# Two scrap tiles, transfers in halves and refitted costs in the planner of a four-layer graph network

## The chip, the cores and the metric

One Trainium2 chip, one core. The time is device microseconds for one execution of the whole program: 2293.68 us before, the median of 3 runs (2291.74 to 2293.85).

## The reference

Thirty-two graphs of 512 nodes with 256 features each (`x`), and a dense 512 x 512 adjacency matrix for each (`adj`), all float32. Four layers run one after the other on each graph; each ends in a residual and a LayerNorm over the features:

```
x = LN(x + gin(x, adj))       # (1+eps) x + adj x, @W1 (256->512), relu, @W2 (512->256)
x = LN(x + gcn(x, adj))       # adj (x W^T + b), leaky with alpha
x = LN(x + graphconv(x, adj)) # h = LN(x); x + relu((adj h) W_rel + b_rel + h W_root)
x = LN(x + gin3(x, adj))      # eps x + adj x, @W1 (256->1024), RMSNorm, silu, @W2 (1024->256)
```

The graphs do not depend on each other. Within a graph nearly everything is one long chain: aggregate, multiply, normalise, and again.

## The kernel before

**Recorded operations.** The kernel does not issue instructions as it walks through the layers. Each helper (`mm`, `act`, `total`, `add`, `copy`, `move` and so on) records an operation in a `Plan` (class at L281), with the tiles that it reads and writes. Because every operation is issued by one closure, all compute instructions carry L366 in the profile and all DMAs L413; tiles tell them apart, not lines.

**The products.** Aggregation (four per graph), both wide layers and most of the narrowing layers are done by a seven-product scheme (`seven`, L846): seven block products into PSUM banks instead of eight, with sums of blocks made on VectorE before, and results added from PSUM to SBUF by VectorE or copied by ScalarE. So VectorE has nearly as much to do as TensorE. A float32 matmul shows as two records.

**The tiles.** SBUF holds 37 `room` tiles of 128 x 1024 (L679), which the planner hands out and takes back; PSUM is eight banks named `ps`; `few` tiles hold the norms' columns. A norm takes, for each of the four chunks of 256 columns of a matrix, a sum (Identity) and a sum of squares (Square) on ScalarE: `Norm.half` (L1177) calls `total` (L735) for them. Only the accumulated column is wanted; the 128 x 256 elementwise output goes to one constant tile `scrap` (L836), which every such operation writes.

**The second layer's bias.** ScalarE writes the bias times the row sum straight into a PSUM bank ahead of the matmuls that accumulate on it (L1421, "seed" in what follows): four 128 x 256 operations per graph.

**The turns.** Where a layer's output comes out transposed (layer 0 in graphs 3 to 28, layer 3 in graphs 1 to 28), VectorE transposes 32 x 32 blocks ("squares") and `spread_squares` (L1272) moves them through DRAM: four writes of 128 KB into a `corner` buffer, then one read of 512 KB back into a room, which VectorE adds to the residual (`add_turned`, L1131). `gather_squares` (L1285) does the like for layer 2, with four writes and four reads of 128 KB. Results leave in one transfer of 512 KB for all but the last two graphs (L1503), which leave in two of 256 KB.

**The order.** `Plan.order` (L479) is a list scheduler that runs when the kernel is built. Up to five graphs are in flight. It gives each operation a rank, which is the graph's number times a period (37) with a shift of its own for some graphs (`SHIFT`), plus when TensorE will need the operation (scaled by a pace, 1.8); the last three graphs follow at 19 instead of 37. Then, step by step, it takes the engine that can start something first, and of what can start there the operation of the lowest rank. When something "can start" comes from a table of assumed costs in us, fitted by hand: busy time and tail of each kind of instruction (L33 to L64), of each kind of DMA (L83 to L87: wire time, and time until landed), a margin `SPARE` after a landing, and a hand-over `HAND` per engine (L93), the time between an instruction's end on one engine and the start of one that waits for it on another. Copies and the scaling at a norm's end may go to VectorE or ScalarE: the planner takes the one that ends first, with `YIELD` (L113) added to VectorE's end. All DMAs go through SyncE's queue in the planner's order; an issue waits until the one eight before has landed (`LANES`). The order within each engine is then fixed, and semaphores do the rest: an instruction that is not ready holds up all that stand behind it on its engine.

Of the kernel before, what the change touches and what calls it, by code (L numbers as in the profile page):

```python
# [12 lines left out]
AF = mybir.ActivationFunctionType  # L13
ALU = mybir.AluOpType

P = 128
# [5 lines left out]
def span(ap):  # L22

    n = 1
    for d in ap.shape[1:]:
        n *= d
    return n
# [28 lines left out]
    return 0.035 + n * 0.00089 + columns * 0.113, 0.105  # L56


def total_time(n, columns):
    return 0.187 + n * 0.00089 + columns * 0.1, 0.1  # L60

# [8 lines left out]

SPARE = 0.8


KEEP = 0.4
# [3 lines left out]
    return 0.1 + kbytes / 450, 1.0  # L80


LOAD, BLOCK = (0.9, 1.7), (0.3, 0.67)  # L83
KEPT, BACK = (0.2, 0.6), (0.35, 0.93)
CORNER, PIECES = (0.46, 0.8), (0.65, 1.05)
TURNED, QUARTER = (2.1, 0.63), (0.58, 0.98)
LINE, SPREAD, RESULT = (0.22, 0.1), (1.47, 0.81), (1.36, 0.8)  # L87

GENTLE = 2.7

HAND = dict(tensor=0.12, vector=0.09, scalar=0.09, gpsimd=0.14, sync=0.1)  # L93
WEIGHTS, AGAIN = 0.09, 0.09


# [13 lines left out]
SOON = 0.03  # L110


YIELD = 0.6  # L113

# [2 lines left out]

RULES = [(37, 1.8, 19, 0.7)]

SHIFT = {-1: -19, 0: 12, 1: 3, 2: 2, 3: -1, 5: 1, 30: -8, 31: -18}
HALVES = 2
AHEAD, LAST = 86.0, 500.0
TURN = {0:(2,3),2:(99,0),3:(0,3)}
ROWS = 1  # L130
ONE = 0
# [149 lines left out]
class Plan:  # L281
# [60 lines left out]
    def do(self, out, *ways, ordered=None, scrap=None, behind=()):  # L342


        ins = list(behind)
        port = False
        def first(x):
            ap = x.model if isinstance(x, Part) else x
            return ap.offset // ap.ap[0][0] if ap.ap[0][0] else 0
        crosses = False  # L350
        for e, method, _, args, kw in ways:
            tiles = [x for x in (*args, *kw.values()) if isinstance(x, (bass.AP, Part))]
            ins += tiles
            in_psum = any(isinstance(x, Part) and x.room.pool.psum for x in tiles)
            crosses |= e == "vector" and any(first(x) != first(out) for x in tiles)
            port |= e == "gpsimd" or method in TWO_OPERANDS and not in_psum

        def issue(engine, method, args, kw):
            def put(x):
                return x.place() if isinstance(x, Part) else x  # L360

            kw = {k: put(x) for k, x in kw.items()}
            if scrap is not None:
                kw["accum_out"] = put(out)
            to = put(out) if scrap is None else scrap
            getattr(getattr(self.nc, engine), method)(to, *(put(x) for x in args), **kw)  # L366

        self.add(
            {
                e: (times, lambda e=e, m=method, args=args, kw=kw: issue(e, m, args, kw))  # L370
                for e, method, times, args, kw in ways
            },
            out, ins, ordered, port, crosses=crosses,
        )
# [267 lines left out]
def tile_gnn_stack(ctx: ExitStack, tc: tile.TileContext, a: dict, out: bass.AP):  # L642
# [33 lines left out]
    HC = NC // 2  # L676
    TH = N // 2
    FH = FC3 // 2
    FLIGHT, ROOMS, SMALL = 5, 37 - ONE, 10  # L679

    const = ctx.enter_context(tc.tile_pool(name="const", bufs=1))
    work = ctx.enter_context(tc.tile_pool(name="work", bufs=1))
# [37 lines left out]
    def scalar(func, n, x, times=scalar_time, **kw):  # L720
        columns = sum(k in ("scale", "bias") and not isinstance(v, float) for k, v in kw.items())
        return "scalar", "activation", times(n, columns), (x,), dict(func=func, **kw)
# [10 lines left out]
        plan.do(o, scalar(func, span(o), x, **kw))  # L733

    def total(o, x, func, **kw):  # L735
        plan.do(o, scalar(func, span(x), x, times=total_time, **kw), scrap=scrap)

    def copy(o, x):
        plan.do(o, scalar(AF.Copy, span(o), x), vector("tensor_copy", span(o), x))
# [38 lines left out]
    def bank(*shape, onto=False, sums=True):  # L778

        n = 1
        for d in shape:
            n *= d
        return Part(Room(banks, sums=n * sums, onto=n * onto)).shaped(*shape)
# [4 lines left out]
    def half(t, h):  # L790
        return t[:, h * HC : (h + 1) * HC]
# [16 lines left out]
    def constant(name, shape):  # L808
        return const.tile(shape, F32, tag=name, name=name)
# [23 lines left out]
    ident = constant("ident", [P, P])  # L833
    make_identity(nc, ident)
    mhalf = constant("mhalf", [P, N // Q])
    scrap = constant("scrap", [P, D])  # L836
    nc.vector.memset(scrap, 0.0)
    nc.vector.memset(mhalf, -0.5)
    pause = constant("pause", [P, 48])
    nc.vector.memset(pause, 0.0)  # L840
# [324 lines left out]
    class Norm:  # L1165
# [33 lines left out]
        def finish(self, h, m, plus, place):  # L1199

            mine = slice(h * HC, (h + 1) * HC)
            ve, rstd, shift = self.ve[:, mine], self.rstd[:, mine], self.shift[:, mine]
            ts(ve, self.squares[:, mine], m / self.n, plus, ALU.mult, ALU.add)
            inv_sqrt(rstd, ve)
            mul(shift, self.less[:, mine], rstd)
            for c in range(h * HC, (h + 1) * HC):
                self.put(c, self.r, rstd[:, c % HC : c % HC + 1], shift[:, c % HC : c % HC + 1])
            plan.move(place, half(self.r, h), (RESULT[0] / 2, RESULT[1]), into=f"out{plan.graph}{h}")

        def put(self, c, y, scale, shift):  # L1210
            r = self.r[:, c, :]
# [60 lines left out]
    def spread_squares(of):  # L1272

        to = room(P // Q, NC * DC * Q)
        of, via = of.whole(P // Q, NC * DC * Q), next(corners)
        names = [f"{via.tensor.name}{a}" for a in range(P // Q)]
        places = via.rearrange("(b i) (a x) -> a i b x", i=Q, a=P // Q)
        for a, name in enumerate(names):  # L1280
            plan.move(places[a], of[a * Q : (a + 1) * Q], CORNER, into=name)
        plan.move(to.whole(N * DC), via, TURNED, outof=names)
        return to

    def gather_squares(to, of):  # L1285
# [64 lines left out]
    def load_x(b):  # L1350
        x = tok()
        src = a["x"][b].rearrange("(p c) d -> p c d", c=NC)
        for h in range(2):
            plan.move(half(x, h), half(src, h), LOAD, gentle=b > 0)
        return x

    def aggregate_first(x, adjacency):
# [40 lines left out]
    def layer1(x, adjacency):  # L1398

        rows = adjacency.row_sums()  # L1400
        aT = aggregate(x, adjacency)
        rs = small(NC)
        by_token(rs, column_sums(rows), 1.0, None, ALU.mult)
        v, neg = tok(), tok()
        norm = Norm(v)

        def done(h):
            act(half(neg, h), half(v, h), AF.Relu, scale=-1.0)
            stt(half(x, h), half(neg, h), nalpha, half(x, h), ALU.mult, ALU.add)
            stt(half(v, h), half(v, h), 0.0, half(x, h), ALU.max, ALU.add)  # L1410
            norm.half(h)

        if ONE:
            for c in range(NC):
                act(v[:, c, :], b_1, AF.Copy, scale=rs[:, c : c + 1])
            dense_add(v, dense_sums(*([halves(aT[:, k : k + 1])] for k in range(DC))), A_1, done, "one")
        for h in range(0 if ONE else 2):
            if SEED:
                ps = dense_tok(
                    [(aT[:, k, :], W_1[:, k, :]) for k in range(DC)], h,  # L1420
                    lambda o, c: plan.do(o, scalar(AF.Copy, D, b_1, scale=rs[:, c : c + 1]), behind=[aT] if BEHINDS else []),  # L1421
                )
                got = ps
            else:
                ps = dense_tok([(aT[:, k, :], W_1[:, k, :]) for k in range(DC)], h)
                for i in range(HC):
                    c = h * HC + i
                    stt(v[:, c, :], b_1, rs[:, c : c + 1], ps[:, i, :], ALU.mult, ALU.add)
                got = half(v, h)
            act(half(neg, h), got, AF.Relu, scale=-1.0)  # L1430
            stt(half(x, h), half(neg, h), nalpha, half(x, h), ALU.mult, ALU.add)
            stt(half(v, h), got, 0.0, half(x, h), ALU.max, ALU.add)
            norm.half(h)

        norm.scales((1.0 + LN_EPS, LN_EPS * LN_EPS), (0.25, 0.25 * LN_EPS))
        h = norm.scaled(0)
        xx = norm.scaled(1)
        u = tok()
        for c in range(NC):
            if ROWS:  # L1440
                act(u[:, c, :], shift_rel, AF.Copy, scale=rs[:, c : c + 1])
            else:
                stt(u[:, c, :], shift_rel, rs[:, c : c + 1], shift_2, ALU.mult, ALU.add)
        if ROWS:
            plus_row(u, shift_2)
        return h, xx, u
# [21 lines left out]
    def layer3(x, adjacency, b):  # L1468
# [27 lines left out]
        if b < B - HALVES:  # L1496
            if turn:
                add_turned(x, dense_turned(right, A2_3, b2c_3), norm.half)
            else:
                dense_add(x, right, A2_3, norm.half)  # L1500
            norm.scales((1.0, LN_EPS))
            y = norm.scaled()
            plan.move(place, y, RESULT, into=f"out{b}", gentle=b < B - 4)  # L1503
        else:

            def done(h):
                norm.half(h)
                norm.finish(h, 1.0, LN_EPS, half(place, h))

            dense_add(x, right, A2_3, done)  # L1510
# [1 line left out]


    plan.graph = -1
    idle, zeros = bank(D), scrap
    for _ in range(9):
        mm(idle, zeros[:, 0:P], zeros, True, True)
    eps0 = row("L0_gnn_eps")
# [2 lines left out]
    loop0 = constant("loop0", [P, P])  # L1521
    ts(loop0, ident, one_eps0, None, ALU.mult)
    plan.graph = 0
    x = load_x(0)
    adjacency = Adjacency(0)
    W1_0 = weight("L0_gnn_W1")
# [83 lines left out]
```

## Time and profile before

| what | value |
|---|---|
| median of 3 runs | 2293.68 us |
| the profiled execution, its own time | 2292.24 us |
| its span, first to last instruction | 2290.4 us |
| granted TensorE clock, mean | 0.999 |
| busy TensorE / VectorE / ScalarE / GpSimd | 2275.2 / 2121.8 / 1762.2 / 240.5 us |
| HBM traffic | 84 GB/s over the span |

A row of a group of instructions reads: line, engine, operation, tile written <- tiles read, shape, count, then busy time, mean duration in ns, and idle time of the engine just before with what ended it. PE is TensorE's matmul, PEld its weight load, DVE VectorE, ACT ScalarE, SPq SyncE's DMA queue. A norm's accumulating operation appears as two records, an ACTIVATE and an ACTIVATION_READ_ACCUMULATOR. Matmuls overlap, so durations add up to more than the time; what counts is the distance from one start to the next.

### The profile page before, as it was taken

The page shows a single profiled execution, that of the slowest core. Times are in us where ns is not written, and L with a number is a line of the kernel's source. Part 1 is how long each engine was busy: PE and PEld are TensorE (multiplying, and loading weights), DVE is VectorE, ACT ScalarE, POOL GpSimd, SP SyncE. Part 2 cuts the span into 40 slices and gives each one's busy share as a digit, 9 for nine tenths or more (in the row PEclk, how much of TensorE's full clock was granted, in tenths as well). Part 3 has the DMA queues.
Part 4 walks back from the last instruction along what each step waited for, and adds up shares of the span by engine and source line. Part 5 has one row for each costly group of instructions (what it writes and reads, how often), then busy time and mean ns, then how long its engine had stood idle before and what let it go on. Part 6 is the DMA issues. An engine that isn't in the chain of part 4 may idle for free.

```text
span 2290.4 us, 37068 instructions
## 1 busy us (share of the span) xinstructions
PE 2275.2 (99%) x11694; PEld 2012.6 (88%) x11694; DVE 2121.8 (93%) x5404; ACT 1762.2 (77%) x4733; POOL 240.5 (11%) x168
## 2 busy tenths in 40 slices
PE   9999999999999999999999999999999999999998
PEld 8889888888888888888888888888888888888888
DVE  8989998999999999999999999999999999998988
ACT  4777778777787777877778877778777887768785
POOL 0000101111011110111100111101111011101111
PEclk9999999999999999999999999999999999999999
DMA  8011322243321333323333223332133331333101
GB/s 246 26 31 40 106 83 75 69 111 106 105 71 54 109 107 106 85 52 94 111 96 112 46 80 111 106 104 77 49 109 109 86 106 51 95 90 84 42 15 61
DMA packets 268404, 195.71 MB, mean 85 GB/s; under 512 B 144560, under 2 KB 224176, under 8 KB 268208
## 3 DMA queue, kind: packets, MB, share of 16 engines
q1 hardware_dynamic: 268208, 193.35, 29.6%
q8 instruction: 93, 1.52, 0.3%
q14 instruction: 103, 0.84, 0.1%
HBM read 124.27 MB, written 69.01 MB: 84 GB/s over the span
## 4 chain that ended last, share of the span: by engine, by line
PE 82%; DVE 8%; ACT 5%; DMA 2%; issue 1%; SPq 1%; POOLq 0%; POOL 0%; DVEq 0%; ACTq 0%
PE ps L366 82%; DVE room L366 7%; ACT room L366 3%; ACT scrap L366 2%; DMA room<-corner 1%; SPq L413 1%; DMA corner<-room 1%; DVE few L366 0%; ACT ps L366 0%; DMA room<-in_x_dram 0%; DVE few L391 0%; DVE A L366 0%; DMA line<-few 0%; POOLq L1606 0%; DVE pause L1571 0%
## 5 line engine op out<-in xcount | busy, mean ns | idle before, releaser
L366 PE MATMUL ps<-room,room 128*128 128x256 f32 (+1 forms) x3572 | 925.9, 381 | 3.5 <-DVE room L366 1.9
L366 DVE TENSOR_TENSOR room<-room,room 128x512 f32<-128x512 f32 (+1 forms) x1486 | 852.1, 601 | 14.7 <-ACT room L366 7.0
L366 PE MATMUL ps<-room,L_gnn_W 128*128 128x256 f32 x2848 | 751.7, 380 | 1.9 <-DVE room L366 1.7
L366 PEld LDWEIGHTS ps<-room,room 128*128 128x128 f32 x3572 | 654.0, 190 | 94.7 <-ACT room L366 8.0
L366 PEld LDWEIGHTS ps<-room,L_gnn_W 128*128 128x128 f32 x2848 | 535.6, 190 | 81.5 <-DVE room L366 5.7
L366 DVE TENSOR_TENSOR room<-ps,room 128x256 f32<-128x256 f32 (+1 forms) x1125 | 528.2, 485 | 70.3 <-PE ps L366 64.6
L366 PE MATMUL ps<-room,A 128*128 128x256 f32 x2136 | 563.6, 379 | 0.3 <-ACT room L366 0.2
L366 ACT ACTIVATE room<-ps,L_gnn_b_c 128x256 f32<-128x256 f32 x984 | 409.8, 469 | 73.6 <-PE ps L366 71.4
L366 POOL TENSOR_TENSOR few<-few,mhalf 128x4 f32<-128x4 f32 (+2 forms) x162 | 239.8, 1481 | 2045.4 <-DVE few L366 1680.8
L366 PEld LDWEIGHTS ps<-room,A 128*128 128x128 f32 x2136 | 403.5, 190 | 56.4 <-ACT room L366 1.9
L366 ACT ACTIVATE room<-ps 128x256 f32<-128x256 f32 (+1 forms) x577 | 227.6, 400 | 244.2 <-PE ps L366 239.2
L366 DVE TENSOR_TENSOR room<-room 128x256 f32<-128x256 f32 (+1 forms) x638 | 311.3, 494 | 16.6 <-ACT room L366 7.3
L366 ACT ACTIVATE scrap<-room,few 128x256 f32<-128x256 f32 x500 | 253.3, 507 | 67.5 <-DVE few L366 61.7
L366 ACT ACTIVATE room<-room,few 128x256 f32<-128x256 f32 x464 | 252.2, 595 | 29.1 <-DVE few L366 28.8
L366 ACT ACTIVATE scrap<-room 128x256 f32<-128x256 f32 x500 | 207.4, 415 | 52.7 <-DVE room L366 43.3
L366 ACT ACTIVATE room<-room 128x1024 f32<-128x1024 f32 x192 | 202.3, 1057 | 48.6 <-DVE room L366 47.6
L366 PE MATMUL ps<-L_gnn_W,room 128*128 128x256 f32 (+1 forms) x960 | 207.6, 331 | 0.7 <-DVE room L366 0.6
L366 ACT ACTIVATE room<-room,L_gnn_rms_weight_c 128x512 f32<-128x512 f32 x256 | 171.7, 722 | 4.2 <-DVE room L366 4.1
L366 PEld LDWEIGHTS ps<-L_gnn_W,room 128*128 128x128 f32 x960 | 156.4, 191 | 17.3 <-ACT ps L366 1.3
L366 PE MATMUL ps<-A,room 128*128 128x128 f32 x1104 | 155.4, 276 | 0.5 <-DVE room L366 0.4
L366 PEld LDWEIGHTS ps<-A,room 128*128 128x128 f32 x1104 | 147.5, 191 | 8.9 <-DVE room L366 2.4
L366 DVE STREAM_TRANSPOSE room<-room 128x512 f32<-128x512 f32 x168 | 113.8, 696 | 1.6 <-ACT room L366 0.5
(62 smaller groups left out, 1221.2 us busy)
## 6 DMA issues: line engine op xcount, KB each, us to landing
corner<-room SPq DMA_DIRECT2D x336, 128.0 KB, 2.5
room<-in_adj_dram SPq DMA_DIRECT2D x128, 256.0 KB, 5.6
room<-corner SPq DMA_DIRECT2D x54, 512.0 KB, 3.8
room<-in_x_dram SPq DMA_DIRECT2D x64, 256.0 KB, 5.8
room<-corner SPq DMA_DIRECT2D x120, 128.0 KB, 3.0
out_dram<-room SPq DMA_DIRECT2D x30, 512.0 KB, 4.7
room<-in_adj_dram SPq DMA_DIRECT2D x128, 64.0 KB, 2.0
diagonal<-room SPq DMA_DIRECT2D x62, 128.0 KB, 2.1
```

The lines of the kernel that those rows point to most:

```text
L366: getattr(getattr(self.nc, engine), method)(to, *(put(x) for x in args), **kw)
L413: getattr(self.nc, engine).dma_start(to, of, **kw)
```

## The change

- `scrap` becomes two tiles, and each accumulating operation takes the next one at the moment at which it is issued, so they alternate in the order in which ScalarE runs them.
- The 512 KB read of a turn becomes two of 256 KB, one for each half of the columns; the first needs only the first two of the four writes. The 512 KB results become two of 256 KB.
- A new cost `seed_time` for the seeds: 0.115 us more than other ScalarE operations.
- 36 rooms instead of 37.
- The assumed costs and the scheduler's constants change: DMA figures, x loads with a figure of their own, 0.05 more in every entry of `HAND`, `SPARE` 1 for 0.8, `YIELD` 0.3 for 0.6, the spacing of the last graphs, `SHIFT`, `AHEAD`.

No operation of the computation is added or dropped. Since the scheduler runs on the new figures, the order changes on every engine.

```diff
+def seed_time(n, columns):
+    return 0.15 + n * 0.00089 + columns * 0.113, 0.105
...
-SPARE = 0.8
+SPARE = 1
...
-LOAD, BLOCK = (0.9, 1.7), (0.3, 0.67)
-KEPT, BACK = (0.2, 0.6), (0.35, 0.93)
-CORNER, PIECES = (0.46, 0.8), (0.65, 1.05)
-TURNED, QUARTER = (2.1, 0.63), (0.58, 0.98)
-LINE, SPREAD, RESULT = (0.22, 0.1), (1.47, 0.81), (1.36, 0.8)
+LOAD, LOAD_X, BLOCK = (0.86, 1.8), (0.67, 1.4), (0.3, 0.66)
+KEPT, BACK = (0.31, 0.5), (0.33, 0.94)
+CORNER, PIECES = (0.43, 0.84), (0.61, 1.09)
+TURNED, QUARTER = (0.75, 1.05), (0.59, 1.05)
+LINE, SPREAD, RESULT = (0.22, 0.1), (1.45, 0.83), (0.66, 1.1)
...
-HAND = dict(tensor=0.12, vector=0.09, scalar=0.09, gpsimd=0.14, sync=0.1)
+HAND = dict(tensor=0.17, vector=0.14, scalar=0.14, gpsimd=0.19, sync=0.15)
...
-YIELD = 0.6
+YIELD = 0.3
...
-RULES = [(37, 1.8, 19, 0.7)]
+RULES = [(37, 1.8, 15, 0.3)]
...
-SHIFT = {-1: -19, 0: 12, 1: 3, 2: 2, 3: -1, 5: 1, 30: -8, 31: -18}
+SHIFT = {-1: -22, 0: 12, 1: 3, 2: 2, 4: -1, 5: -3, 30: -4, 31: -5}
 HALVES = 2
-AHEAD, LAST = 86.0, 500.0
+AHEAD, LAST = 72.0, 500.0
...
-            to = put(out) if scrap is None else scrap
+            to = put(out) if scrap is None else next(scrap)
...
-    FLIGHT, ROOMS, SMALL = 5, 37 - ONE, 10
+    FLIGHT, ROOMS, SMALL = 5, 36, 10
...
-    scrap = constant("scrap", [P, D])
-    nc.vector.memset(scrap, 0.0)
+    scraps = [constant(f"scrap{i}", [P, D]) for i in range(2)]
+    nc.vector.memset(scraps[0], 0.0)
...
-        plan.move(to.whole(N * DC), via, TURNED, outof=names)
+        for h in range(2):
+            mine = slice(h * N * DC // 2, (h + 1) * N * DC // 2)
+            plan.move(to.whole(N * DC)[:, mine], via[:, mine], TURNED, outof=names[2 * h : 2 * h + 2])
...
-            plan.move(half(x, h), half(src, h), LOAD, gentle=b > 0)
+            plan.move(half(x, h), half(src, h), LOAD_X, gentle=b > 0)
...
-            plan.move(place, y, RESULT, into=f"out{b}", gentle=b < B - 4)
+            for h in range(2):
+                plan.move(half(place, h), half(y, h), RESULT, into=f"out{b}{h}", gentle=b < B - 4)
...
+    scraps = cycle(scraps)
```

More of the change, by code (lines that the diff above doesn't have):

```diff
@@ L735, in total @@
     def total(o, x, func, **kw):
-        plan.do(o, scalar(func, span(x), x, times=total_time, **kw), scrap=scrap)
+        plan.do(o, scalar(func, span(x), x, times=total_time, **kw), scrap=scraps)
     def copy(o, x):
@@ L1207, in finish @@
                 self.put(c, self.r, rstd[:, c % HC : c % HC + 1], shift[:, c % HC : c % HC + 1])
-            plan.move(place, half(self.r, h), (RESULT[0] / 2, RESULT[1]), into=f"out{plan.graph}{h}")
+            plan.move(place, half(self.r, h), RESULT, into=f"out{plan.graph}{h}")
         def put(self, c, y, scale, shift):
@@ L1420, in layer1 @@
                     [(aT[:, k, :], W_1[:, k, :]) for k in range(DC)], h,
-                    lambda o, c: plan.do(o, scalar(AF.Copy, D, b_1, scale=rs[:, c : c + 1]), behind=[aT] if BEHINDS else []),
+                    lambda o, c: plan.do(o, scalar(AF.Copy, D, b_1, times=seed_time, scale=rs[:, c : c + 1]), behind=[aT] if BEHINDS else []),
                 )
@@ L1514, in tile_gnn_stack @@
     plan.graph = -1
-    idle, zeros = bank(D), scrap
+    idle, zeros = bank(D), scraps[0]
     for _ in range(9):
```

## The prediction

> **What bounds the kernel now.** I read the page's shares first, then the table of stretches, then TensorE's timeline at its fullest and where it stops, then the waits.
>
> ```profile
> PE 2275.2 (99%) x11694; PEld 2012.6 (88%) x11694; DVE 2121.8 (93%) x5404; ACT 1762.2 (77%) x4733; POOL 240.5 (11%) x168
> 1000.00:1025.00 25.00, 25.00 (x117) 21.99 (x117) 24.45 (x53) 22.91 (x62) 1.64 (x1) 1.00 0.01 1
> ```
>
> TensorE is never out of work for long. The second line is a stretch of 25 us (columns: PE, PEld, DVE, ACT, POOL busy with counts, granted clock, DMA share, GB/s): 117 matmul records at a full clock, 0.214 us each, while VectorE has 24.45 of 25 us filled. But "busy" hides short gaps, because matmul durations overlap; the timeline shows starts.
>
> ```profile
> 2276.94 0.39 PE L366 MATMUL ps<-L_gnn_W,room 128*128 128x128 f32 x2
> 2277.16 0.39 PE L366 MATMUL ps<-A,room 128*128 128x128 f32 x2
> ...
> 613.26 0.59 PE L366 MATMUL ps<-room,room 128*128 128x256 f32 x2
> 613.69 0.59 PE L366 MATMUL ps<-room,L_gnn_W 128*128 128x256 f32 x2
> 614.65 0.70 PE L366 MATMUL ps<-room,L_gnn_W 128*128 128x256 f32 x2 [0.37 <-DVE room L366]
> ```
>
> Two records of 128 columns take 0.22 us from start to start, two of 256 columns 0.43 (42 of them between 604.62 and 613.69: 0.216 each). At 613.69 the next start comes 0.96 later instead of 0.43: a loss of 0.53. By shape the program has 9078 records of 256 columns, 2600 of 128 and 16 of 512: 9078 x 0.216 + 2600 x 0.112 + 16 x 0.432 = 2258.9 us of TensorE that the change does not touch. The rest of the span of 2290.4 is: 1.2 before the first matmul; 2.9 more than the cadence in the warm-up matmuls on `scrap` (18 records from 1.2 to 7.95); 7.2 from the last matmul (2283.2) to the end, a norm and an output; and what is left, 20.2, is lost in small gaps. Summing the gaps over 0.03 us in the timeline directly gives 22.0 in 156 places. I take 21: this is all that the change can win, 0.9% of the time. By place: 2.9 in 8 to 150 us (21 gaps), 10.1 in 150 to 1950 (73), 9.0 in 1950 to 2283 (62), where few graphs are left to fill in.
>
> ```profile
> PEld ps L366 <- DVE room L366: 14.5, 38, 1.5
> PEld ps L366 <- ACT room L366: 13.5, 44, 0.8
> ```
>
> The waits of the weight loads (total us, times, longest; loads run ahead, so these exceed the loss) say that VectorE and ScalarE end about half each. Where the five largest gaps in mid-kernel lie (263.9, 614.7, 966.8, 1325.0, 1671.9; losses 0.71, 0.53, 0.60, 1.47, 0.88, together 4.2), the chain of waits has a `room<-corner` read of 512 KB, then VectorE, then TensorE: at 614.7 a read from 610.33 that took 3.06, at 1325 one of 5.77.
>
> **The change, part by part.**
>
> Two scrap tiles. ScalarE's timeline:
>
> ```profile
> 1028.16 0.49 ACT L366 ACTIVATE scrap<-room,few 128x256 f32<-128x256 f32 x1
> 1028.56 0.19 ACT L366 ACTIVATION_READ_ACCUMULATOR scrap<-room,few 128x1 f32 x1
> 1028.78 0.51 ACT L366 ACTIVATE scrap<-room,few 128x256 f32<-128x256 f32 x1
> 1029.19 0.19 ACT L366 ACTIVATION_READ_ACCUMULATOR scrap<-room,few 128x1 f32 x1
> 1029.28 0.82 ACT L366 ACTIVATE room<-ps,L_gnn_b_c 128x256 f32<-128x256 f32 x2
> ```
>
> After the first accumulator read the next scrap writer comes 0.22 later; after the second, ahead of another kind of operation, 0.09. The difference, 0.13, is a wait on ScalarE's own last write to the same tile. 401 of the 1000 pairs show it: 401 x 0.126 = 50 us of ScalarE. In the order of the changed kernel only one scrap writer still waits for the operation directly before it, against 423. ScalarE is 77% busy, so none of the 50 us is on the path by itself. But the planner assumes 0.415 (0.515 with a bias column), and ran 0.52 to 0.62: in a half norm of four such operations it fell up to 4 x 0.11 behind the plan, and all behind it. That goes; next to be late there is VectorE, which ends the other half of the waits. Bounds: nothing, if ScalarE's lateness came from what it waited for, to all that ScalarE-ended gaps hold after the next item (about 6.5). I take -3.
>
> `HAND` + 0.05, `SPARE` + 0.2. They leave each step more air, so an instruction which the plan starts exactly when ready is started less often too early. Of the 156 gaps, 123 are under 0.1; the sum of the first 0.05 of each is 7.6 us, 3.5 of it between 150 and 1950, 4.1 at both ends. In the middle other graphs' matmuls can fill the air: all of 3.5. At the ends the planner has less to put there: half. Together -5.6; bounds 0 to -7.6.
>
> Halves. 54 reads become 108, 30 results 60: 84 more issues at 0.41 = 34 us of SyncE, which waits most of the time. In the order of the changed kernel 19 of the 54 first halves stand eight issues behind the fourth write (result halves, a load and layer 2's quarters come first), where 23 stood five behind before; 23 follow the fourth write directly. Each waits at the head of SyncE's queue for its two writes, and behind it stand the next graph's loads, of which only one ended a TensorE gap before (0.54 at 2027.6). VectorE's add needs both halves, so the second one counts.
>
> ```profile
> room<-corner SPq DMA_DIRECT2D x54, 512.0 KB, 3.8
> room<-corner SPq DMA_DIRECT2D x120, 128.0 KB, 3.0
> ```
>
> Between these rows 256 KB lands in an estimated 3.3, so the second half lands at 0.41 + 3.3 = 3.7, at best 0.1 sooner than the whole. [...] The row's fixed part (2.7 by the two rows) makes the split worth nothing[...]. For the five gaps [...]the rows 0.5; three more issues ahead in 19 places would cost 1.2 each where one is late. Bounds -4.2 to +4; the 0.2 of `SPARE` weighs on the good side: -1.5.
>
> Seeds. The rows give 477 ns into PSUM, 499 for the same operation into SBUF (`room<-shift_rel`), but pairs of seeds start 0.49 apart, since the second waits for the first. The plan had 0.376 busy. 128 seeds with 0.115 more: a truer plan, counted in the items above.
>
> `YIELD` 0.3. By the counts of both programs 91 scalings and 37 copies go from ScalarE to VectorE: 91 x 0.32 + 37 x 0.33 (starts in VectorE's timeline) = 41.7 us, less 45 pause memsets at 0.175 = 7.9: +33.8 on VectorE, -91 x 0.49 - 37 x 0.26 = -54 on ScalarE. VectorE idles 164 us in all; that cover shrinks by a fifth. What waits for VectorE is TensorE. Left of its share of the gaps is about 6: a fifth to a quarter more is +1.6. Upper bound below.
>
> One room less, `AHEAD`, the last graphs' spacing. Loads wait longer for a room; by that one gap, 0 to +3: +1. The reordered tail could go either way by some 3 of its 9: 0.
>
> Sum: 21 - 3 - 5.6 - 1.5 + 1.6 + 1 = 13.5. Span 2258.9 + 1.2 + 2.9 + 7.2 + 13.5 = 2283.7, 6.7 less than 2290.4. The profiled execution took 1.8 more than its span and the median of the runs is 1.4 above that: 2287.0.
>
> **The rivals.**
>
> VectorE becomes the late one (slower). 38 of the 91 full stretches of 25 us have it at 24.0 or more; the one shown has 0.55 to spare. The moved work is 41.7 / 91 = 0.46 a stretch. From two more operations in such a stretch (0.65) it no longer fits, and each lateness reaches TensorE directly. If moved work falls evenly, 42% of 41.7 = 17.5 is uncovered: 13.5 + 17.5 = 31, median 2304; with part of it caught, 2301. For: VectorE ends the longer waits. Against: the stretches beside them have 2 to 4 us free, and ScalarE gets shorter at the same time.
>
> The plan gets truer but the gaps are not about it (no change): new gaps take the place of old ones, because each order is new everywhere and its gaps fall by chance. Then 21 stays about 21: 2290 to 2297. For: the longest gaps come from colliding transfers, which one figure for each kind can't see. Against: 123 of 156 gaps are under 0.1, the size of a hand-over.
>
> **How the numbers follow.** 0.2% (4.6 us) is about what a measurement can tell from no change. The likeliest case, 2278 to 2291, 0.58 (0.52 faster, 0.06 within); no change 0.17 (0.02, 0.13, 0.02 slower); VectorE late 0.25 (0.22 slower, 0.03 within). Faster 0.54, same 0.22, slower 0.24. The range ends low where nearly all gaps of the middle and half of the tail's go (13.5 - 9), and high in the VectorE case: 2278 to 2302.
>
> **What would show it.** Right: accumulator reads followed by a scrap writer at 0.09; ScalarE-ended weight load waits well under 13.5 us; PE gaps under 0.1 fewer than half as many; VectorE at about 2156 (by starts) to 2170 us (by durations). Wrong: stretches with VectorE at 24.9 and PE below 24.8, which is the first rival; or losses at reads of a corner half, with the issue late behind others; or a head or tail (before 150, after 1950) that loses more than 12 us.

## The result and the profile after

The changed kernel takes 2285.89 us (median of 10 runs, 2282.45 to 2287.93) against 2291.56 for the kernel before (10 runs in the same rounds): ratio 0.9973, 95% interval 0.9963 to 0.9982, 5.7 us less. The profiled execution took 2287.09 with a span of 2285.3.

The page's first part, and the same stretch of 25 us that the prediction shows of the kernel before:

```profile
PE 2268.2 (99%) x11694; PEld 2020.3 (88%) x11694; DVE 2151.9 (94%) x5487; ACT 1690.4 (74%) x4605; POOL 239.9 (10%) x168
1000.00:1025.00 25.00, 25.00 (x118) 22.00 (x117) 23.89 (x58) 22.83 (x63) 2.65 (x2) 1.00 0.15 27
```

TensorE has the same 11694 records. VectorE gained 30 us of work, ScalarE lost 72, of which the operations that moved are 68 (91 x 0.595 + 37 x 0.375 by their rows of before). The waits between scrap writers (the accumulating operations, whose elementwise output goes to `scrap`) lie between the records and are not in these sums; ScalarE's timeline shows them gone:

```profile
1016.21 0.50 ACT L370 ACTIVATE scrap<-room,few 128x256 f32<-128x256 f32 x1
1016.61 0.20 ACT L370 ACTIVATION_READ_ACCUMULATOR scrap<-room,few 128x1 f32 x1
1016.70 0.50 ACT L370 ACTIVATE scrap<-room,few 128x256 f32<-128x256 f32 x1
1017.10 0.19 ACT L370 ACTIVATION_READ_ACCUMULATOR scrap<-room,few 128x1 f32 x1
```

The next scrap writer comes 0.09 after the accumulator read, not 0.22. Of all reads followed by a scrap writer without an idle gap, 401 were at about 0.22 before and none are now (481 at 0.09). The weight loads' waits:

```profile
PEld ps L370 <- DVE room L370: 10.1, 23, 2.7
PEld ps L370 <- ACT room L370: 4.6, 9, 2.3
```

Waits that ScalarE ends fell from 13.5 us in 44 places to 4.6 in 9. The table counts TensorE's lost time as the prediction did: what lies between two matmul starts beyond the cadence of the first, where that is over 0.03 us. It is split by how much matmul work was done by then, so that the parts stay comparable when orders shift. "Loss" in what follows means these columns, in this order:

| kernel, profiled | head (8 to 150 us of work) | 150 to 400 | middle (400 to 1920) | tail | all | gaps of 0.10 or less (rounded) | last matmul to end |
|---|---|---|---|---|---|---|---|
| before | 3.1 | 2.8 | 7.3 | 9.1 | 22.3 | 123 | 7.2 |
| changed | 0.7 | 0.5 | 8.1 | 6.4 | 15.7 | 50 | 9.0 |

So 6.6 us of gaps went, all of them before 400 and after 1920; the middle gained nothing, and the end after the last matmul grew by 1.8 (there the timeline has eight result transfers issued from 2276.18 on, where it had four from 2282.98). New long gaps came, here in TensorE's timeline:

```profile
539.79 1.03 PE L370 MATMUL ps<-room,room 128*128 128x256 f32 x4
542.69 1.99 PE L370 MATMUL ps<-room,room 128*128 128x256 f32 x8 [1.87 <-ACT room L370]
...
1951.80 1.89 PE L370 MATMUL ps<-room,room 128*128 128x256 f32 x8
1956.03 2.47 PE L370 MATMUL ps<-room,room 128*128 128x256 f32 x5 [2.34 <-DMA room<-in_x_dram]
```

At 0.216 each, the four records from 539.79 should be followed at 540.65, and the next start is at 542.69: 2.0 lost. The eight from 1951.80 should be followed at 1953.53: 2.5 lost. The chain of waits (start, length, what) shows what stood behind the second:

```profile
1942.92 0.24 SPq L417
...
1943.25 6.01 DMA room<-in_adj_dram
...
1949.28 6.62 DMA room<-in_x_dram
...
1956.03 1.19 PE ps L370 x2
```

An x load was issued only when an adjacency load eight places ahead of it had landed, and TensorE waited for it. Ahead of the gap at 542.7 the chain has a diagonal write of 3.25 us, then VectorE, then ScalarE. The reads of the corners:

```profile
room<-corner SPq DMA_DIRECT2D x108, 256.0 KB, 3.4
...
room<-corner SPq DMA_DIRECT2D x120, 128.0 KB, 4.8
```

A half lands in 3.4, where the whole took 3.8; but layer 2's quarters went from 3.0 to 4.8. The halves as such do not explain that: in six kernels below that also have halves the quarters stay at 3.0 to 3.2, while with whole transfers and the changed figures they take 4.0. It goes with the order of the issues.

### The profile page after: what moved, and what is told of

The parts are those of the page before. It is cut to its first block, busy times and chain, and to the rows that moved or that the text cites. A ratio compares the mean times of both kernels' runs of the same rounds, so it can differ in the third digit from the quotient of the medians.

```text
span 2285.3 us, 37266 instructions
## 1 busy us (share of the span) xinstructions
PE 2268.2 (99%) x11694; PEld 2020.3 (88%) x11694; DVE 2151.9 (94%) x5487; ACT 1690.4 (74%) x4605; POOL 239.9 (10%) x168
## 4 chain that ended last, share of the span: by engine, by line
PE 94%; DMA 3%; DVE 2%; issue 1%; ACT 0%; SPq 0%; POOL 0%; POOLq 0%; DVEq 0%
PE ps L370 94%; DMA room<-in_adj_dram 2%; DVE room L370 2%; DMA room<-in_x_dram 1%; DMA room<-corner 0%; ACT room L370 0%; SPq L417 0%; DMA diagonal<-room 0%; DVE few L370 0%; DVE few L395 0%; POOL few L370 0%; DVE A L370 0%; DVE L_gnn_W_root L370 0%; POOLq L1614 0%; DVE shift L370 0%
## 5 line engine op out<-in xcount | busy, mean ns | idle before, releaser
L370 POOL TENSOR_TENSOR few<-few,mhalf 128x4 f32<-128x4 f32 (+3 forms) x162 | 239.2, 1478 | 2040.5 <-DVE few L370 1760.8
L370 ACT ACTIVATE room<-ps 128x256 f32<-128x256 f32 (+1 forms) x540 | 216.4, 405 | 174.0 <-PE ps L370 172.2
L370 ACT ACTIVATE room<-room,few 128x256 f32<-128x256 f32 x373 | 205.0, 597 | 109.1 <-DVE few L370 108.9
```

## The experiments

Each kernel was run beside the kernel before on the same chip, and ratios are to that (the median of before lay between 2288.5 and 2292.3 on these chips, so kernels of different groups are compared by ratios). Losses come from each one's own profiled execution and are given as in the table: head, 150 to 400, middle, tail.

**One room less alone.** The kernel before with this edit:

```diff
-    FLIGHT, ROOMS, SMALL = 5, 37 - ONE, 10
+    FLIGHT, ROOMS, SMALL = 5, 36, 10
```

> The kernel before with 36 rooms instead of 37, all else as it was (two scrap tiles and 37 rooms do not fit into the memory together). The prediction gave one room less 0 to +3 us. If only the number of rooms matters: +1 (ratio 1.0004). If every new order has gaps of its own by chance: anywhere within 0.998 to 1.002 of before.

Measured: 1.0099 (1.0085 to 1.0112), 22.6 us slower, far outside both. The loss is 18.7, 3.5, 7.2 and 12.6 (42.0 in all): most of it is new in the head, and the middle is as before. The waits show one long gap that was not there:

```profile
PEld ps L366 <- POOL few L366: 9.6, 1, 9.6
PE ps L366 <- POOL few L366: 9.2, 1, 9.2
```

It is where graph 0 turns its row norms by TensorE (`everywhere`, L1301): TensorE's queue stands for 9.2 us at transposes that wait for GpSimd's power (which makes the norms' factors), which takes 1.0 itself and came that late:

```profile
144.94 1.01 POOL L366 TENSOR_TENSOR few<-few,mhalf 128x4 f32<-128x4 f32 x1 [27.06 <-DVE few L391]
```

GpSimd in turn had waited 27 us for VectorE, which was at work without a break until just before. So the gap was made by what the queues held in the new order, and no row names a late load; why the planner put the transposes there was not tried.

**Two scraps in that order.** The same with two scrap tiles, as in the change. The order of every engine is instruction for instruction that of the kernel above.

> The kernel before with 36 rooms and two alternating scrap tiles; instruction for instruction the same order as with 36 rooms and one scrap, so only the waits of scrap writers on each other differ. My theory: about 3 us faster than with one scrap (ratio to before about 0.9990), fewer TensorE gaps ended by ScalarE. Rival (ScalarE has 23% of its time free and its lateness comes from elsewhere): the same as with one scrap within 1 us.

Measured: 1.0042 (1.0028 to 1.0056), 12.6 us faster than the kernel above by medians. The middle's loss goes from 7.2 to 1.9 and the tail's from 12.6 to 9.2; the head's 18.5, GpSimd's gap with it, stays. The theory's mechanism holds and its size is four times mine.

**One scrap in the changed kernel's order.**

```diff
-    scraps = cycle(scraps)
+    scraps = cycle(scraps[:1])
```

> The changed kernel with one scrap tile again, in the same order. My theory: ScalarE falls behind the plan again in each half norm, about 3 us slower than the changed kernel (ratio to before about 0.9985). Rival (the hand-over margin alone covers it): as the changed kernel, 0.9973, within 0.0005.

Measured: 0.9998 (0.9989 to 1.0007). The gain of the whole change is gone with this one line. The order is that of the changed kernel, 479 accumulator reads are again followed by a scrap writer at about 0.22 and none at 0.09, the loss goes from 15.7 to 23.1 (middle 8.1 to 13.3), and ScalarE is back at the weight loads:

```profile
PEld ps L370 <- DVE room L370: 13.7, 27, 2.6
PEld ps L370 <- ACT room L370: 11.6, 28, 2.7
```

Everything else in the change, the room, the halves, the refitted figures, nets to nothing within the 2 us of the interval.

**The margins alone.** The kernel before with the new `HAND` and `SPARE` lines of the diff.

> The kernel before with only the hand-over margins 0.05 higher and SPARE 1 for 0.8. My theory: about 5.6 us faster (ratio 0.9976), TensorE gaps under 0.1 us cut to less than half of 123. Rival (gaps fall by chance in every new order): 0.998 to 1.002 and no fewer small gaps.

Measured: 1.0005 (0.9996 to 1.0014): no gain. In the stretches (PE busy and records are the columns to read; the third is the middle):

```profile
8.00:150.00 142.00, 137.79 (x752) 118.82 (x751) 133.11 (x363) 96.74 (x268) 8.36 (x7) 1.00 0.37 108
...
400.00:1950.00 1550.00, 1549.78 (x7769) 1378.82 (x7769) 1446.25 (x3620) 1247.66 (x3344) 167.36 (x110) 1.00 0.32 91
```

In the middle 7769 records fit where the kernel before had 7743: loss 1.8 against 7.3. In the head TensorE is busy 137.8 of 142 against 141.3: loss 7.9 against 3.1, and the tail has 10.2. Small gaps fall to 83, not below half. The margins did what was expected where other graphs fill in, more so than expected, and made the ends worse by as much.

**The margins taken out of the changed kernel.** `HAND` and `SPARE` as before.

> The changed kernel with the old hand-over margins and SPARE 0.8. After the margins alone took 5.7 us of gaps out of the stretch from 400 to 1950 us but gave them back before 400 and after 1950: with two scrap tiles the margins are worth about 3 us in the middle, so this is some 3 us slower than the changed kernel (ratio to before 0.9985). Rival (the two scrap tiles already make the plan true, the margins add nothing): 0.9973 within 0.0010.

Measured: 1.0048 (1.0035 to 1.0060), 17 us over the changed kernel by the ratios (0.0075 x 2290). Loss 33.4: 5.6, 10.5, 10.6 and 6.7. Both expectations were wrong on size: the lost time is mainly before 400, with GpSimd's gap again (2.9 us at 164).

**Whole transfers.** The changed kernel with `TURNED` at (2.1, 0.63), one read per turn and one transfer per result, as before the change.

> The changed kernel with the turns' reads and the results in whole transfers of 512 KB and their old figures, 84 issues fewer; all else as changed. My theory (halves worth nothing or a little less than nothing; the changed kernel still loses 8.0 us in gaps between 400 and 1950, where two scrap tiles alone left 1.9): 0 to 4 us faster, ratio to before 0.9955 to 0.9973. Rival (the halves are what keeps the long gaps short): 2 to 6 us slower, ratio 0.998 to 1.000.

Measured: 0.9989 (0.9980 to 0.9998). The loss is the same as with halves, 15.2 against 15.7; by the ratios the halves are ahead by some 4 us, but the two intervals overlap, and the orders of all engines but GpSimd differ. It settles nothing about halves.

**VectorE's handicap.** The changed kernel with `YIELD` at 0.6.

> The changed kernel with YIELD 0.6 again, so fewer scalings and copies on VectorE. If the work moved to VectorE makes the gaps of 0.3 to 0.7 us at the fourth aggregation (5 places between 600 and 1610): 2 to 4 us faster, ratio to before 0.9955 to 0.9965. The prediction's own price for it was 1.6 us. Rival (ScalarE would be the late one without it): 2 us or more slower.

Measured: 1.0011 (1.0002 to 1.0020), 9 us slower than the changed kernel by the ratios. VectorE is at 2118.9, 33 us less, as counted. The middle is better (5.5 against 8.1), the tail too (2.3 against 6.4), but 4.3 is lost in the head and 10.1 from 150 to 400. So it is the rival expectation whose size came. Before 400, TensorE's own waits are ended by ScalarE for 4.4 us in four places, by VectorE for 2.1 in three and by GpSimd for 2.0 in one.

**The old pacing.** The changed kernel with `RULES`, `SHIFT` and `AHEAD` as before.

> The changed kernel with the old spacing of the last graphs, shifts and look-ahead (RULES, SHIFT, AHEAD as before). My theory now: these set the losses at both ends, where the changed kernel loses 1.1 us before 400 us against 5.6 before the change; so 4 us or more slower than the changed kernel, ratio to before 0.999 or more, the loss before 400 and after 1950. Rival (the ends follow the margins): as the changed kernel within 0.0010.

Measured: 1.0066 (1.0053 to 1.0078), 21 us slower than the changed kernel by the ratios. From its stretches, and the same of the changed kernel:

```profile
150.00:400.00 250.00, 239.22 (x1223) 211.57 (x1222) 226.12 (x576) 174.32 (x468) 25.30 (x17) 0.99 0.24 69
400.00:1950.00 1550.00, 1549.65 (x7773) 1380.01 (x7773) 1470.93 (x3820) 1167.06 (x3209) 166.22 (x110) 1.00 0.32 90
```

```profile
150.00:400.00 250.00, 250.00 (x1294) 222.89 (x1293) 236.92 (x602) 184.92 (x494) 25.41 (x17) 1.00 0.28 76
400.00:1950.00 1550.00, 1546.26 (x7740) 1375.06 (x7740) 1465.77 (x3703) 1180.35 (x3225) 166.22 (x110) 1.00 0.32 90
```

The middle is nearly free of gaps (7773 records against 7740, a loss of 0.9 against 8.1), while 14.5 is lost from 150 to 400 and 15.6 in the tail. So the pacing figures buy the ends, and here the middle pays for them.

**Which pacing figure.** The changed kernel with the fourth figure of `RULES` at 0.7, and with `AHEAD` at 86.

> The changed kernel with the fourth pacing figure at 0.7 as before (how far operations that feed no matmul directly are put off). With all old pacing the middle lost only 0.9 us, with the changed pacing 8.1. If this figure is what makes the middle, the middle falls to about 1 and the time to 4 to 6 us under the changed kernel, ratio to before 0.995, unless the head (before 400) is lost by it, as with all old pacing (17.7): then ratio 1.000 to 1.003. If the look-ahead makes the middle: as the changed kernel, 0.9973, middle about 8.

> The changed kernel with the look-ahead at 86 as before instead of 72. If the look-ahead makes the middle: middle about 1 us of gaps, ratio to before about 0.995, or up to 1.003 if the head is lost by it. If the fourth pacing figure does: middle about 8, ratio about 0.9973.

Measured: 0.9999 (0.9990 to 1.0008) and 1.0012 (1.0003 to 1.0021). The look-ahead makes the middle: loss 0.9 with 86, 5.3 with the other figure at 0.7, 8.1 as changed. Both lose it again before 400: 9.8 (the figure at 0.7) and 16.0 (look-ahead 86) there against 1.2. The guess of 0.995 failed for both; what came is its fallback, 1.000 to 1.003 if the part before 400 is lost.

**The scraps by themselves.** The kernel before, its 37 rooms and its order kept. The 37 rooms leave no space for a second full scrap tile, so two of half the bytes take the place of the one, and the warm-up matmuls read their zeros from a room.

```diff
-    scrap = constant("scrap", [P, D])
-    nc.vector.memset(scrap, 0.0)
+    scraps = [const.tile([P, D], mybir.dt.bfloat16, tag=f"scrap{i}", name=f"scrap{i}") for i in range(2)]
+    zero = rooms.tiles[-1][:, 0:D]
+    nc.vector.memset(zero, 0.0)
```

> The kernel before with two alternating scrap tiles of half the width in bytes (bfloat16, only the thrown-away output is rounded), so 37 rooms still fit; the order of every engine is that of the kernel before, to the instruction (the warm-up matmuls read zeros from a room). Theory (the two scraps alone are the gain, all else in the change nets to nothing): 5 to 6 us faster, ratio 0.9973 to 0.9980, and the gaps of 7.3 us between 400 and 1920 us of work fall to about 2, as they did with 36 rooms. Rival (the scraps pay only in an order made for them): ratio 0.999 to 1.000.

Measured: 0.9963 (0.9949 to 0.9976), 8.8 us by medians: the scraps alone give what the whole change gave (0.9973, the intervals overlap), if not more. The loss is 10.5 (2.1, 0.5, 5.1, 2.7) against 22.3; the profiled execution was the fastest of its five. The middle fell less than the 2 expected. The waits of the weight loads:

```profile
PEld ps L366 <- DVE room L366: 8.6, 21, 1.3
...
PEld ps L366 <- ACT room L366: 2.9, 9, 0.8
```

The VectorE-ended waits fell too, from 14.5: much of VectorE's lateness was ScalarE's, one step on. VectorE's own waits for sums from scrap writers show that step, the kernel before first, this one second:

```profile
DVE few L366 <- ACT scrap L366: 19.0, 28, 2.0
```

```profile
DVE few L366 <- ACT scrap L366: 11.2, 13, 1.9
```

What is left in the middle are four gaps at the old places of the 512 KB reads (617, 966, 1320, 1667; together 3.4).

**Halves by themselves.** The same with each turn's read issued as two halves at the place of the whole:

```diff
+            if times is TURNED:
+                n = of.shape[1] // 2
+                for h in range(2):
+                    mine = slice(h * n, (h + 1) * n)
+                    self.nc.sync.dma_start(to[:, mine], of[:, mine])
+                return
             getattr(self.nc, engine).dma_start(to, of, **kw)
```

> The kernel before with 37 rooms and two narrow scrap tiles, order unchanged, and the 54 reads of 512 KB issued as two of 256 KB one behind the other at the place where the whole stood (54 issues more; results stay whole; the planner's figures untouched). It measures the halves by themselves against the same kernel with whole reads (ratio 0.9963 to before). By the rows of before (the second half lands 0.1 us sooner at best): within 0.0004 of 0.9963, the last half landing about 3.7 us after the first issue against 3.8. [...] If the extra issues and the reuse of DMA lanes hold up the queue: 1 to 4 us slower, 0.997 to 0.998, with more loss at the reads (617, 965, 1320, 1667 us).

Measured: 0.9941 (0.9928 to 0.9955), 2278.60 us: the fastest of all, faster than both kernels, and better than each of the expectations. Against whole reads the intervals overlap a little, so the halves' own share is not clear of noise; by the profiles the loss falls by 1.8 (middle 5.1 to 3.5), by the ratios 5 us. The DMA rows, this kernel's first and the whole reads' second:

```profile
room<-corner SPq DMA_DIRECT2D x108, 256.0 KB, 3.5
```

```profile
room<-corner SPq DMA_DIRECT2D x54, 512.0 KB, 3.7
```

The second half is issued a median 0.51 after the first and lands 4.3 after the first issue, 0.6 later than the whole; so an earlier landing does not explain a gain. Nor do the waits for reads from `corner`: VectorE's fell from 4.6 us in 7 places to 3.4 in 5, but ScalarE's rose from 1.8 in one to 3.5 in two. In this order the halves do no harm that shows; whether they help, and by what, stays open.

## Why the prediction was right, and where its steps were not

The forecast was 0.29% less and 0.27% came. The total was right, and the mechanism of the two scraps; most of the other terms were not, and that they added up to the right total was in part luck. The terms of the sum, one by one:

- **The signs named beforehand** came: accumulator reads at 0.09, ScalarE-ended waits of 4.6 against 13.5, small gaps 50 against 123; VectorE, at 2152, a little under the 2156 named. (The added work sums to 41.3 and 33.4, not 41.7 and 33.8.)
- **The ceiling** held: 21 us of gaps to win, the matmul work untouched. The gaps went from 22.3 to 15.7, to 13.3 by the remainder that the sum used (last matmul at 2276.3, less 1.2, 2258.9 and 2.9); the sum said 13.5. By that remainder the kernel before had 20.2, so 6.9 went, where the sum took 7.5 off 21.
- **The end.** The sum kept 7.2 after the last matmul, and 9.0 came. The time still fits because the median of the runs lies 1.2 under the profiled execution here, where the sum added 1.4: luck.
- **Two scraps, -3.** The mechanism was right and the size too small. In the order of the changed kernel it is 5.7 us (0.9998 against 0.9973), in that of the kernel before 8.8, in that with 36 rooms 12.6. I had capped it at the gaps that ScalarE ends and given the margins first claim on them; the runs show that VectorE-ended gaps go with it (14.5 to 8.6 in the weight loads' waits), since VectorE waits for the sums.
- **Margins, -5.6.** Wrong as a saving of its own: +0.05% alone. The middle gave 5.4 us, more than the 3.5 of the estimate, but the ends, set at half a gain, lost 6.2 and the end after the last matmul 1.2.
- **Halves, -1.5.** More than its own working gave: the rows' price was 0.5 over the five gaps, and `SPARE`, which it leans on, was already counted with the margins. In place the gain is 1.8 us by the profiles and 5 by the ratios, not clear of noise, and the last half lands later, not 0.1 sooner.
- **VectorE, +1.6.** The added work came (30 us), the first rival did not: in 36 of the 91 full stretches VectorE is at 24.0 or more, against 38, and in none at 24.9 with TensorE below 24.8. The cost was not seen: moving the work back made the kernel slower, by losses before 400.
- **One room less, +1.** Wrong by a factor of twenty if it stands alone: 22.6 us, most of it at the transposes of graph 0, and the waits there name no load.
- **Pacing and the last graphs, 0.** Undoing it costs 21 us, though the middle gains 7.2 by it. That the new pacing makes up for the lost room is likely but not shown: no run has one of them without the other figures.

So the errors cancelled: the margins' saving that did not come against the scraps' that was twice as large; the room's cost, it seems, against the pacing's gain. The second rival, that each new order has gaps of its own by chance, was nearer to the truth for everything but the scraps: everything else together moved the time by nothing (0.9998), while undoing single parts of it cost 4 to 21 us each (the 4, of the halves, not clear of noise). Those undo prices add up to far more than the change gave, so they are not shares of its gain; they suggest that the figures had been fitted to each other. What stays open is why the part before 400 responds so strongly; the runs only show one place, the transposes of graph 0 that wait for GpSimd's power, in five of the kernels that lose there. The new DMA figures, the cost of the seeds and the 37th room in the changed kernel were not tried by themselves.

## What to carry to other kernels

An output that nobody reads is still a write, and if all of one engine's operations share it, each waits for the last: give it two tiles, narrow ones if memory is short, before touching the schedule. Where a planner fixes the order from assumed costs, a part that changes a cost and a part that changes a figure of the plan can't be summed: test the first in an unchanged order, and the second as a whole. And look at the head, the middle and the tail apart, since a truer figure can win in the middle and lose at both ends.

## What the runs showed of the hardware

- An accumulating ScalarE operation that waits for its predecessor's write to the same tile starts 0.13 us later than one that does not (0.22 against 0.09 after the accumulator read), and writes of bfloat16 take as long as of float32 (median 407 ns in both, with two tiles).
- Reads of 256 KB from DRAM into a room landed in 3.1 to 3.5 us (the medians of eight kernels), those of 512 KB in 3.6 to 3.9 (of six). So two halves issued 0.51 apart landed later than one whole: 4.3 against 3.7.
- With a DMA issued only when the one eight before it has landed, one slow load holds up another: an x load was issued at 1949.28, when an adjacency load of 6.01 us had landed at 1949.26, and TensorE lost 2.5 us.
